# Blocks of 64 slots on two halves of the array's columns, in a two-layer graph network with routed experts

## The chip, the cores and the metric

The kernel runs on 1 core of one Trainium2 chip. The metric is the device time of one launch in microseconds (us); the time of a kernel is the median of its runs. The profile is one separately recorded execution; its span goes from the first to the last instruction on the core.

The engines are called as in the profile: PE (TensorE, matrix products and transposes), PEld (its weight loads), DVE (VectorE), ACT (ScalarE), POOL (GpSimd) and SP (SyncE, which only issues transfers). An engine's name with a q (SPq, ACTq, POOLq) stands for the instructions with which it issues DMAs.

## What is computed

N = 625 tokens of D = 768 numbers pass through two layers. Each layer adds to x a graph part and an attention part, and then the output of routed experts:

```python
edge_index = jnp.stack([src, dst])                     # 10000 edges, 8 types
xn = layernorm(x)
x = x + L0_gnn(xn, edge_index, edge_type_8) + L0_mix(xn)     # two relational convolutions; linear attention
x = x + L0_ffn(layernorm(x))                                 # 8 experts, 768-192-384-768, two of them per token
xn = layernorm(x)
x = x + L1_gnn(xn, edge_index) + L1_mix(xn)                  # two graph attentions; linear attention
x = x + L1_ffn(layernorm(x))                                 # 8 experts, 768-1152-768, two of them per token

# one relational convolution: mean over the incoming edges of each type, then a product per type
mean = segment_sum(x[src], dst * 8 + etype) / max(count, 1)
out = einsum('nri,rio->no', mean.reshape(N, 8, -1), W) + x @ root + b

# the experts (layer 1; layer 0 has two hidden layers and a bias on its scores)
probs, idx = top_k(softmax(x @ router_w + router_b), 2)
out = sum over e of gates[:, e] * (gelu(x @ w1[e] + b1[e]) @ w2[e] + b2[e])
```

All products are fp32, but for the neighbour sums, in which x is split into three bf16 parts.

## The kernel before

**Common parts.** Tokens stand as NB = 5 groups of T = 125. All matrix products write PSUM tiles called `ps`, [128, 2, 512] fp32, of which there are four in turn; `evac(dst, ps, i)` copies one out, on ACT for even i and on DVE for odd i (on ACT that is the line L163). `wpool` has five buffers named `w` for weight slabs of 1152 KB, loaded on SP's queue by `slabs` and `slab_tiles`; a load waits until an older slab's buffer is free, and what is queued behind it on SP waits too. Four large buffers (`work`, `features`, x's own, and `pair` of the relational layers) are used for one thing after another. Contents that are needed later are stored to `aside_d` in DRAM and read back by `recall` on ACT's queue (L981): `hid` (L808, SP's queue) in the first relational layer, x (L1124, SP's queue) in the second.

**Relational layers.** `rgcn` (from L847) is called twice, once per convolution. For each of seven relations it makes six neighbour-sum tiles (L853: bf16 products of the parts of x with the table of edge counts), scales and mixes them on DVE (L882 to L888), mixes quarters of the weight matrix on POOL (L874 to L878), and makes Strassen's seven products of half-size matrices. Each of the seven has three column slices of 128, so there are 21 products u of three steps of k each (L900), two of which share a PSUM tile: 11 tiles per relation, u0 = 0, 2, ..., 20. For relation 0 a tile is copied by `evac(total, ps, u0 // 2)`, so ACT and DVE alternate; for the others DVE adds it to the totals (L906). Totals 0 to 11 lie in `sums`, totals 12 to 20 in `more`, the first half of `pair`. `sums` overlays `place(2)`: in the first convolution that is `work`, which holds `hid` until L808 has stored it; in the second it is x's buffer, which holds x until L1124 has stored it. The eighth relation and the root product go through plain products; before them eight DVE operations (L921 to L931) combine the totals m1 to m7, and the last of them to read `sums` (L924, which the trace has behind L925) precedes the recall into `work` (`acc = back()`).

`counts` (L826 to L836) builds in the first layer the tile `cnt` of edge counts on POOL's queue, and stores it on ACT's queue (L834) for the second layer. ACT's queue is in order with ACT's own copies: where L834 waits for `cnt`, so do the copies behind it.

**Experts.** `Dispatch` (L360 to L435) gives each (token, expert) pair a slot. It ranks the tokens of each expert, counts the blocks of 128 slots that an expert needs (`nblk`, from the comparison of the expert's count with `steps` = 0, 128, ..., 512), gives each expert its first block (`first`), and writes for every block the expert (`es_i`), the token row of every slot (`idx`) and, in `gates`, the weight of every slot. These are products of one-hot tables, with one column per block. All this stands between the last score (L305, L431 is the last of its DVE operations that the first gather needs) and the first gather. NS = 17 blocks are enough for any routing; the first NU = 13 are run always, the other four in a branch, taken only if the chip counts more than 13 (L1217 in layer 0, L1520 in layer 1).

A block of layer 0 (`block0`, L1160 to L1203) loads its expert's weights on SP (`w12` for w1 and w2, three buffers; w3 in a `w` buffer), gathers 128 token rows (POOL), transposes them, and makes three products with transposes and a Gelu between them; its rows are multiplied by the gates and added to the sums in DRAM by an indirect DMA on POOL. `blocks0` runs the six steps of the blocks in a staggered order, each block three steps behind the one before. A block of layer 1 (`block1`, L1485 to L1517) takes three slabs of w1 (pool `moe`, six buffers) and three of w2 (`w`, five buffers), makes the first product in three column groups of 384 (L1498, 18 products), copies each out (L1501), transposes it, applies Gelu on ACT, and makes the second product in two column groups (L1511, 18 products). Blocks run one after the other.

In the attention of layer 0, the products L757 and L772 already write the two halves of the output partitions (0 to 63 and 64 to 127) in turn, each from a stationary of 64 columns.

The functions that the change touches, and what calls them:

## Time and profile before

| | |
|---|---|
| median of 3 runs | 2432.52 us (2432.51 to 2446.29) |
| the profiled execution | 2438.95 us, span 2437.2 us, mean granted clock 0.968 |
| busy PE / DVE / ACT / POOL | 93% / 38% / 12% / 19% of the span |
| DMA | 313.13 MB, mean 128 GB/s |
| neighbour sums, L853 | 2880 products, 391.6 us |
| relational products, L900 | 504 products, 138.8 us |
| expert products of layer 1, L1498 and L1511 | 468 each, 160.3 and 155.2 us |
| gathers of expert blocks, L487 | 26 (13 per layer) |

How to read the profile: the span is cut into 40 equal slices, and a row of digits gives the busy share of an engine in each, in tenths; the row DMA is the mean share of the core's 16 DMA engines. In a row of a timeline the first two numbers are the start in the span and the duration in us, followed by engine, line, operation, output <- inputs, partitions x elements and type, and the number of instructions that were merged (x16); [0.94 <-ACT xT L163] is the engine's idle time before it and what ended it. In a table of windows a row gives the stretch, the length and the sum over engines, and then the busy time and number of instructions of PE, PEld, DVE, ACT, POOL and SP; its last three columns are the mean granted clock, the busy share of the DMA engines and the GB/s that they moved. An fp32 product appears as two instructions (passes), so L1498's 468 products of 384 columns are 13 blocks times 18 products times two passes.

### The profile page before, as it was taken

The page shows a single profiled execution, that of the slowest core. Times are in us where ns is not written, and L with a number is a line of the kernel's source. Part 1 is how long each engine was busy: PE and PEld are TensorE (multiplying, and loading weights), DVE is VectorE, ACT ScalarE, POOL GpSimd, SP SyncE. Part 2 cuts the span into 40 slices and gives each one's busy share as a digit, 9 for nine tenths or more (in the row PEclk, how much of TensorE's full clock was granted, in tenths as well). Part 3 has the DMA queues.
Part 4 walks back from the last instruction along what each step waited for, and adds up shares of the span by engine and source line. Part 5 has one row for each costly group of instructions (what it writes and reads, how often), then busy time and mean ns, then how long its engine had stood idle before and what let it go on. Part 6 is the DMA issues. An engine that isn't in the chain of part 4 may idle for free. (4 is left out here: it accounts for less than half of the span.)

```text
span 2437.2 us, 24793 instructions
## 1 busy us (share of the span) xinstructions
PE 2270.4 (93%) x10116; PEld 1506.7 (62%) x10116; DVE 931.3 (38%) x1902; ACT 284.4 (12%) x583; POOL 467.0 (19%) x257
## 2 busy tenths in 40 slices
PE   7999979999999999999999797899999996999997
PEld 4666557777776567777776564455676554555554
DVE  7554143344334233344433422614673534211110
ACT  2111000000001000000000112213551201111110
POOL 1676532232220022222200121000000200010010
PEclk9999999999999999999999698999999998999998
DMA  9435395444422051111100997011003201988783
GB/s 360 84 53 55 76 249 139 122 129 134 131 61 77 12 183 60 62 58 53 33 32 26 296 312 205 13 71 72 1 24 105 72 13 31 396 319 314 275 310 120
DMA packets 153022, 313.13 MB, mean 128 GB/s; under 512 B 49070, under 2 KB 69938, under 8 KB 152864
## 3 DMA queue, kind: packets, MB, share of 16 engines
q1 hardware_dynamic: 91784, 234.38, 27.4%
q0 software_dynamic: 52384, 51.64, 10.9%
q10 hardware_dynamic: 8728, 25.38, 3.1%
q8 instruction: 85, 1.39, 0.2%
q14 instruction: 41, 0.34, 0.0%
HBM read 250.27 MB, written 64.76 MB: 129 GB/s over the span
## 5 line engine op out<-in xcount | busy, mean ns | idle before, releaser
L853 PE MATMUL ps<-cnt,parts 125*128 125x314 bf16 x2880 | 391.6, 299 | 7.2 <-DVEq L1038 4.9
L853 PEld LDWEIGHTS <-parts 125*128 125x128 bf16 x2880 | 283.0, 98 | 115.4 <-issue 10.5
L609 POOL DMA_INDIRECT table<-val,idx x80 | 162.2, 2028 | 132.8 <-DMA table<-val,idx 58.4
L1498 PE MATMUL ps<-w,xT 128*128 128x384 f32 x468 | 160.3, 493 | 13.2 <-ACT xT L163 6.6
L1511 PE MATMUL ps<-w,hT 128*128 128x384 f32 x468 | 155.2, 486 | 0.0
L900 PE MATMUL ps<-pair,w 128*128 128x314 f32 x504 | 138.8, 434 | 7.6 <-ACT work L163 7.6
L874 POOL TENSOR_TENSOR features<-w 128x1152 f32<-128x1152 f32 x14 | 37.3, 2666 | 526.0 <-issue 352.4
L487 POOL DMA_INDIRECT xg<-tokens,d_idx x26 | 26.3, 1011 | 544.3 <-PE ps L499 252.3
L1498 PEld LDWEIGHTS ps<-w,xT 128*128 128x128 f32 x468 | 86.7, 192 | 69.0 <-ACT xT L163 8.4
L900 PEld LDWEIGHTS ps<-pair,w 128*128 128x128 f32 x504 | 97.2, 193 | 46.9 <-ACT work L163 8.1
L1511 PEld LDWEIGHTS ps<-w,hT 128*128 128x128 f32 x468 | 87.8, 190 | 58.3
L187 PE MATMUL ps<-w,hT 128*125 128x384 f32 x360 | 117.8, 486 | 0.0
L187 PEld LDWEIGHTS ps<-w,hT 128*125 128x125 f32 x360 | 67.1, 188 | 46.9
L163 ACT COPY features<-ps 128x628 f32<-128x628 f32 (+1 forms) x15 | 10.5, 703 | 729.7 <-PE ps L853 728.9
L1312 PE MATMUL ps<-xl,pT 125*125 125x256 f32 (+1 forms) x300 | 81.0, 426 | 12.7 <-ACT pT L163 8.8
L906 DVE TENSOR_TENSOR pair<-ps,pair 128x628 f32<-128x628 f32 (+1 forms) x60 | 44.8, 746 | 122.7 <-PE ps L900 122.7
L822 PE MATMUL ps<-w,features 128*125 128x384 f32 x240 | 82.7, 503 | 0.0
L1501 DVE COPY a<-ps 128x384 f32<-128x384 f32 x39 | 21.7, 557 | 151.2 <-PE ps L1498 151.2
L187 PE MATMUL ps<-w,features 128*125 128x384 f32 x240 | 79.3, 490 | 0.0
L1424 POOL TENSOR_TENSOR row<-row 128x768 f32<-128x768 f32 x1 | 1.9, 1918 | 401.7 <-ACT z L1295 401.7
L1312 PEld LDWEIGHTS ps<-xl,pT 125*125 125x125 f32 x300 | 56.2, 191 | 34.4 <-ACT pT L163 10.3
L196 PE MATMUL ps<-features,w 128*128 128x313 f32 x288 | 77.4, 427 | 0.0
(374 smaller groups left out, 3349.8 us busy)
## 6 DMA issues: line engine op xcount, KB each, us to landing
w<-in_L_ffn_w_dram SPq DMA_DIRECT2D x78, 1152.0 KB
w<-in_L_gnn_W_dram SPq DMA_DIRECT2D x34, 1152.0 KB
w<-in_L_ffn_W_dram SPq DMA_DIRECT2D x13, 1152.0 KB
table<-zero SPq DMA_DIRECT2D x32, 400.0 KB
cnt<-table POOLq DMA_DIRECT2D x16, 800.0 KB, 7.9
edges<-cnt POOLq DMA_DIRECT2D x8, 1600.0 KB, 15.9
w<-in_L_ffn_W_dram SPq DMA_DIRECT2D x13, 576.0 KB
w<-in_L_mix_W_qkv_dram SPq DMA_DIRECT2D x6, 1152.0 KB
```

The costliest lines, as they stand in the source:

```text
L187: nc.tensor.matmul(ps[:T, h, :width], xT[:, k, blk(b)], w_of(k)[:, h * width : (h + 1) * width], start=(k == 0), stop=(k == nk - 1))
L196: nc.tensor.matmul(ps[:width, h, :NH], w_of(k)[:, c0 : c0 + width], xT[:, k, h * NH : (h + 1) * NH], start=(k == 0), stop=(k == nk - 1))
L487: nc.gpsimd.indirect_dma_start(out=dst, out_offset=None, in_=table_d, in_offset=bass.IndirectOffsetOnAxis(ap=rows, axis=0))
L609: scatter = nc.gpsimd.indirect_dma_start(out=table_of(g, j), out_offset=bass.IndirectOffsetOnAxis(ap=idx[:, j : j + 1], axis=0), in_=val[: ...
L822: nc.tensor.matmul(ps[:T, h, :384], aggs[:, k, blk(b)], w_of(k)[:, h * 384 : (h + 1) * 384], start=(k == 0), stop=(k == KC - 1))
L853: nc.tensor.matmul(ps[:, h, :HC], parts[:, b, i, k * 128 : (k + 1) * 128], cnt[:T, b, h * HC : (h + 1) * HC], start=(b == 0 and i == 0), s ...
L874: nc.gpsimd.tensor_add(wmix[:, 1], b11, b12)
L900: nc.tensor.matmul(ps[:, j, :HC], right[:, k, c : c + 128], left(k), start=(k == 0), stop=(k == K2 - 1))
L906: nc.vector.tensor_add(total, ps[:, :n, :HC], total)
L1312: nc.tensor.matmul(o, pT[:, j, :], xl[:, j, cols], start=(j == 0), stop=(j == NB - 1))
L1498: nc.tensor.matmul(ps[:, 0, :384], xT[:, k, :], w1_of(k)[:, q * 384 : (q + 1) * 384], start=(k == 0), stop=(k == KC - 1))
L1511: nc.tensor.matmul(ps[:, h, :384], hT[:, k, :], w2_of(k)[:, h * 384 : (h + 1) * 384], start=(k == 0), stop=(k == 8))
```

## The change

Blocks of two kinds. `steps` now begins at 64, so an expert whose last, partial block holds up to 64 slots gets a half block for it (numbers 13 to 20), and a whole block (0 to 12) where it holds more. `nblk`, `first` and `last` have two rows, one per kind, and `jump` and `rest` move the slots of a rest to their half block's number. The lists are written out: ten whole blocks and three half blocks (13, 14, 15) are always run, in the order RUN; the other three whole and five half blocks (MORE) in the branch, which is taken if the chip counts more than ten whole or more than three half blocks. The tables of blocks have 21 columns for 17.

A half block uses 64 slots as stationary and gives the array's two column halves two different groups of output columns, so the results stand on partitions 0 to 63 and 64 to 127. Its output tile has 128 rows of 384 numbers, and its scatter adds to half rows of the sums, with addresses `idx2`; the products that make `idx2` and the half blocks' gates are repeated for both halves. In layer 0 half blocks take part in the staggered order; in layer 1 the half block's first product comes between its whole neighbour's first and second product, and its own second product after that.

Relational layers. Totals 0 to 8 now go to `more` (in `pair`), totals 9 to 20 to `sums`, and the tiles are u0 = 0, 2, 4, 6, 8 (one product), 9, 11, ..., 19. For relation 0 `evac` gets u0, so the first five tiles go to ACT and the other six to DVE. The store of x before the second convolution is issued on ACT's queue, not SP's.

```diff
-NU = 13
-NS = 17
+NPB = 13
+NHB = 8
+NS = NPB + NHB
+RUN = (0, 1, 2, 13, 3, 4, 5, 14, 6, 7, 8, 15, 9)
+MORE = (10, 11, 12, 16, 17, 18, 19, 20)
+NUP, NUH = 10, 3
...
+            nblk = pool.tile([128, 2, 8], F32, name="d_nblk", bufs=1)
+            nc.vector.tensor_reduce(nblk[:, 0, :], over, AX.X, OP.add)
+            whole = pool.tile([128, 8], F32, name="d_whole", bufs=1)
+            nc.vector.tensor_scalar(whole, nblk[:, 0, :], 128.0, None, op0=OP.mult)
+            nc.vector.tensor_tensor(nblk[:, 1, :], rank[:, NB, :], whole, op=OP.is_gt)
...
+            jump = pool.tile([128, 8], F32, name="d_jump", bufs=1)
+            nc.vector.tensor_sub(jump, first[:, 1, :], nblk[:, 0, :])
+            nc.vector.scalar_tensor_tensor(jump, jump, float(NPB), first[:, 0, :], op0=OP.add, op1=OP.subtract)
+            rest = pool.tile([T, NB, 8], F32, name="d_rest", bufs=1)
+            nc.vector.tensor_tensor(rest, rank[:T, :NB, :], whole[:T, None, :].to_broadcast([T, NB, 8]), op=OP.is_ge)
+            nc.vector.tensor_mul(rest, rest, jump[:T, None, :].to_broadcast([T, NB, 8]))
+            nc.vector.tensor_add(rest, rest, first[:T, 0, None, :].to_broadcast([T, NB, 8]))
             pos = pool.tile([T, NB, 8], F32, name="d_pos", bufs=1)
...
+            nc.vector.scalar_tensor_tensor(pos, rest, 128.0, rank[:T, :NB, :], op0=OP.mult, op1=OP.add)
...
+            for h in (slice(0, 64), slice(64, 128)):
+                for c in range(2 * NB):
+                    nc.tensor.matmul(ps[h, 1, : 2 * NHB].rearrange("p (i s) -> p i s", i=2), lane_hot[:, c, :64],
+                                     put[:, :, c // NB, c % NB, NPB:], start=(c == 0), stop=(c == 2 * NB - 1))
...
+            behind(nc.vector.tensor_scalar(many, last[0:1, 0, 7:8], float(NUP), None, op0=OP.is_gt))
+            behind(nc.vector.scalar_tensor_tensor(self.used, last[0:1, 1, 7:8], float(NUH), many, op0=OP.is_gt, op1=OP.add))
...
+            behind(nc.vector.scalar_tensor_tensor(self.idx2, ps[:, 1, :NHB], 2.0, row2, op0=OP.mult, op1=OP.add))
...
+    def half_rows(table_d):
+        return table_d.rearrange("r (h d) -> (r h) d", h=2)
+    sides = [slice(0, 64), slice(64, 128)]
+    def half_slot_columns(src):
+        ps = ps_tile()
+        sl = ps.rearrange("p a c -> p (a c)")[:, : KC * 64].rearrange("p (k c) -> p k c", c=64)
+        for k in range(KC):
+            nc.tensor.transpose(sl[:, k, :], src[:, k * 128 : (k + 1) * 128], ident[:64, :64])
+        return sl
...
-            def of_product(i):
-                return sums[:, 3 * i : 3 * i + 3, :] if i < 4 else more[:, 3 * i - 12 : 3 * i - 9, :]
+            def of_products(u0, n):
+                return more[:, u0 : u0 + n, :] if u0 < 9 else sums[:, u0 - 9 : u0 - 9 + n, :]
...
-                for u0 in range(0, 21, 2):
+                for u0 in (0, 2, 4, 6, 8, 9, 11, 13, 15, 17, 19):
...
-                    n = min(2, 21 - u0)
+                    n = 1 if u0 == 8 else 2
...
-                    total = sums[:, u0 : u0 + n, :] if u0 < 12 else more[:, u0 - 12 : u0 - 12 + n, :]
+                    total = of_products(u0, n)
                     if r == 0:
-                        evac(total, ps[:, :n, :HC], u0 // 2)
+                        evac(total, ps[:, :n, :HC], u0)
...
-            nc.sync.dma_start(by_token(aside_d[2]), x)
+            nc.scalar.dma_start(by_token(aside_d[2]), x)
...
+            def block0_half(b, w1, w2, w3):
+                i = b - NPB
+                xg = moe.tile([128, D], F32, name="xg", bufs=4)[:64]
+                gather(xg, tokens_d[0], idx[:64, b : b + 1])
+                xT = moe.tile([128, KC, 128], F32, name="xT", bufs=3)[:, :, :64]
+                evac(xT, half_slot_columns(xg), b)
...
+                for k in range(KC):
+                    for j, p in enumerate(sides):
+                        nc.tensor.matmul(ps[p, 0, :96], xT[:, k, :], w1[:, k, j * 96 : (j + 1) * 96],
+                                         start=(k == 0), stop=(k == KC - 1))
+                a1 = moe.tile([128, 192], F32, name="a1")
+                nc.vector.tensor_copy(a1[:, :96], ps[:, 0, :96])
...
+                for k in range(2):
+                    for p, c in zip(sides, (slice(0, 256), slice(256, 384))):
+                        nc.tensor.matmul(ps[p, 0, : c.stop - c.start], h1[:96, k, :64], w2[:, k, c],
+                                         start=(k == 0), stop=(k == 1))
...
+                y = moe.tile([128, D], F32, name="y")[:, :384]
+                ps = ps_tile()
+                for k in range(3):
+                    for j, p in enumerate(sides):
+                        nc.tensor.matmul(ps[p, 0, :384], h2[:, k, :64], w3[:, k, j * 384 : (j + 1) * 384],
+                                         start=(k == 0), stop=(k == 2))
...
+                nc.vector.tensor_scalar(y, ps[:, 0, :384], gates[1][:, i : i + 1], None, op0=OP.mult)
+                scatter_add(half_rows(sums_d[0]), y, places_of.idx2[:, i : i + 1])
...
-            blocks0(range(NU))
+            blocks0(RUN)
             w1_of = slabs(a["L1_gnn_W1"], 1024, 2)
-            with tc.If(nc.values_load(used, min_val=0, max_val=NS) > NU):
-                blocks0(range(NU, NS), moe)
+            with tc.If(nc.values_load(used, min_val=0, max_val=2) > 0):
+                blocks0(MORE, moe)
...
+                i = b - NPB
+                gather(xg[:64], tokens_d[1], idx[:64, b : b + 1])
+                evac(xT[:, :, :64], half_slot_columns(xg[:64]), b)
+                ps = ps_tile()
+                for k in range(KC):
+                    for h in range(2):
+                        for p, c in zip(sides, (slice(h * 320, (h + 1) * 320), slice(640 + h * 256, 896 + h * 256))):
+                            nc.tensor.matmul(ps[p, h, : c.stop - c.start], xT[:, k, :64], w1_of(k)[:, c],
+                                             start=(k == 0), stop=(k == KC - 1))
+                a1 = moe.tile([128, 640], F32, name="a1_half", bufs=1)
+                nc.vector.tensor_copy(halves(a1[64:, :512]), ps[64:, :, :256])
+                nc.vector.tensor_copy(halves(a1[:64, :]), ps[:64, :, :320])
+                ps = ps_tile()
+                for c in range(4):
+                    nc.tensor.transpose(ps[:, 0, c * 128 : (c + 1) * 128], a1[:, c * 128 : (c + 1) * 128], ident)
+                nc.tensor.transpose(ps[:, 1, :64], a1[:64, 512:640], ident[:64, :64])
+                for c in range(9):
+                    at = ps[:, 1, :64] if c == 4 else ps[:, 0, c % 5 * 128 + c // 5 * 64 :][:, :64]
+                    nc.scalar.activation(hT[:, c, :64], at, AF.Gelu, bias=c1[:, b, c : c + 1])
+                yield
+                ps = ps_tile()
+                for k in range(9):
+                    for j, p in enumerate(sides):
+                        nc.tensor.matmul(ps[p, 0, :384], hT[:, k, :64], w2_of(k)[:, j * 384 : (j + 1) * 384],
                                          start=(k == 0), stop=(k == 8))
                 if not gates:
-                    gates.append(gate())
-                nc.vector.tensor_scalar(halves(y), ps[:, :, :384], gates[0][:, b : b + 1], None, op0=OP.mult)
-                scatter_add(sums_d[1], y, idx[:, b : b + 1])
-
-            for b in range(NU):
-                block1(b)
-            with tc.If(nc.values_load(used, min_val=0, max_val=NS) > NU):
-                for b in range(NU, NS):
-                    block1(b)
+                    gates.extend(gate())
+                nc.vector.tensor_scalar(y[:, :384], ps[:, 0, :384], gates[1][:, i : i + 1], None, op0=OP.mult)
+                scatter_add(half_rows(sums_d[1]), y[:, :384], places_of.idx2[:, i : i + 1])
+            def blocks1(bs):
+                run = {b: block1(b) for b in bs}
+                for i, b in enumerate(bs):
+                    if b < NPB or i == 0:
+                        next(run[b])
+                        within = i + 1 < len(bs) and b < NPB <= bs[i + 1]
+                        if within:
+                            next(run[bs[i + 1]])
+                        next(run[b], None)
+                        if within:
+                            next(run[bs[i + 1]], None)
+                    elif bs[i - 1] >= NPB:
+                        next(run[b])
+                        next(run[b], None)
+            blocks1(RUN)
+            with tc.If(nc.values_load(used, min_val=0, max_val=2) > 0):
+                blocks1(MORE)
```

## The prediction

> **What bounds the kernel now.** I read the page's engine and slice rows, then the windows of the two expert stages, the timeline there and at the starts of the relational layers, and the rows of the attention products that already use halves of the array.
>
> ```profile
> PE 2270.4 (93%) x10116; PEld 1506.7 (62%) x10116; DVE 931.3 (38%) x1902; ACT 284.4 (12%) x583; POOL 467.0 (19%) x257
> PE   7999979999999999999999797899999996999997
> DMA  9435395444422051111100997011003201988783
> ```
> TensorE is the bound nearly throughout, so what shortens its stream or removes one of its waits counts. DMA is also full in two stretches: the first expert stage (1362 to 1503 us) and the second (2077 to 2420).
>
> ```profile
> 1440.00:1445.00 5.00, 5.00 (x21) 3.35 (x21) 0.36 (x1) 0.00 (x0) 0.00 (x0) 1.00 1.06 313
> 2150.00:2155.00 5.00, 5.00 (x17) 2.94 (x16) 0.00 (x0) 0.00 (x0) 0.00 (x0) 1.00 0.31 83
> 2155.00:2160.00 5.00, 3.68 (x16) 2.26 (x15) 1.88 (x2) 0.00 (x0) 1.44 (x2) 1.00 0.96 378
> 2170.00:2175.00 5.00, 5.00 (x19) 3.03 (x18) 0.56 (x1) 1.06 (x4) 0.00 (x0) 1.00 1.03 413
> 2175.00:2180.00 5.00, 5.00 (x17) 2.95 (x16) 0.00 (x0) 0.00 (x0) 0.00 (x0) 1.00 0.14 52
> ```
> The last three columns are clock, DMA share and GB/s. In the first stage DMA is never idle; in the second it rests for some 5 us of every 26, waiting for a weight buffer (five `w` tiles; a block takes three for w2).
>
> ```profile
> 2132.85 5.43 PE L1498 MATMUL ps<-w,xT 128*128 128x384 f32 x16 [0.94 <-ACT xT L163]
> 2146.84 10.49 PE L1511 MATMUL ps<-w,hT 128*128 128x384 f32 x32
> 2395.49 5.43 PE L1498 MATMUL ps<-w,xT 128*128 128x384 f32 x16 [0.94 <-ACT xT L163]
> 133.84 2.33 PE L772 MATMUL ps<-phi_q,kv 128*64 128x313 f32 x16 [0.23 <-DVE kv L766]
> 145.19 2.38 PE L757 MATMUL ps<-phi_k,x 125*64 125x256 f32 x20
> ```
> A second-stage block lasts (2395.49 - 2132.85)/10 = 26.3 us. An fp32 product is two passes; L1511's 32 passes give (10.49 - 0.49)/31 = 0.323 us for 384 columns, 0.84 ns a column. L772 and L757 write the two halves of the output partitions in turn, from 64-column stationaries. Less the last pass's duration, L772 takes (2.33 - 0.43)/15 = 0.127 us per 313-column pass, where 0.263 would be serial; L757 (2.38 - 0.38)/19 = 0.105 against 0.215. So two halves overlap fully.
>
> ```profile
> 355.57 3.34 PE L900 MATMUL ps<-pair,w 128*128 128x314 f32 x12
> 365.75 0.68 ACT L163 COPY work<-ps 128x628 f32<-128x628 f32 x1 [136.71 <-DMA aside<-work]
> 365.78 0.33 ACTq L834 DMA_DIRECT2D counts<-cnt  x1
> 366.49 9.54 PE L900 MATMUL ps<-pair,w 128*128 128x314 f32 x24 [7.58 <-ACT work L163]
> 847.57 0.30 SPq L1124 DMA_DIRECT2D aside<-x  x1
> 868.02 2.67 POOL L874 TENSOR_TENSOR features<-w 128x1152 f32<-128x1152 f32 x1 [173.58 <-DMA w<-in_L_gnn_W_dram]
> 883.09 6.71 PE L900 MATMUL ps<-work,w 128*128 128x314 f32 x18 [3.20 <-POOL w L877]
> ```
> First relational layer: four PSUM tiles are full at 358.9 and none can be emptied, since `sums` overlays `work`, whose store lands at 365.7. Second: TensorE waits 3.2 us for mixed weights that landed late behind the store of x.
>
> **How many blocks there will be.** Evaluating the reference's routers on its inputs gives, per expert, 0, 366, 6, 167, 0, 2, 624, 85 slots in the first layer and 0, 0, 1, 579, 0, 262, 408, 0 in the second. In 128s that is 13 blocks each, as the trace has it (L1202 and L1515 x13). With rests up to 64 taken as halves it is 10 whole and 3 half blocks in both layers: exactly the unconditional list, so the conditional one stays untaken.
>
> **Second expert stage.** A half block's first product has 6 k x 2 x 2 passes of 320 columns beside 256 in the other half: 24 x 0.269 = 6.5 us. The second: 18 x 0.323 = 5.8. Eleven transposes (a whole block's fifteen take 0.82 + 3 x 0.49 = 2.3): 1.4. The wait for xT, as now: 1.0. Changes between whole and halved array: some six at 0.1 (L757's last pass starts near 147.19, full-array L196 at 147.50, 0.1 beyond that pass's 0.215): 0.6. Sum 15.3, so 11.0 less than 26.3, three times: -32.9. Without changes of array and with shorter transposes it is 14.6 (-35); with 0.2 us for each of seven changes and 1.9 us for two DVE copies that nothing covers, 18 (-25). Weight bytes stay. A whole block and its half are queued on SP with six w2 tiles; the sixth, and the next block's w1 behind it, waits until the whole block has read w2's first tile for the last time, two thirds through its second product (S2). From there to the next first product is 4 + 5.8 + 2 = 12 us; the queue owes four tiles of 1.18 MB by then, 2.95 us each at 400 GB/s plus some 3 us to land (L353's load issued at 1513.77 is read at 1517.48), and the scatter's traffic: 14.6 to 16.6 us; the last tile is needed 2.6 us in, at 14.6. So a stall of 0 to 2 us per pair: +3 (0 to +6). On POOL the half block's scatter follows the whole one's by 6 us, and a scatter lands in 8.9, so POOL waits some 3 us; the gathers behind it run a block ahead: 0. Net -30.
>
> **First expert stage.** Ten blocks from 1388.8 to 1489.1 are 10.0 us each. Half block: L1180's products are 12 pairs of 96 columns, 0.081 us of streaming, but two weight loads (L757's loads come every 0.096 us): 1.8 for now 1.9. w2 4 x 0.215 = 0.9 (1.3); w3 6 x 0.323 = 1.9 (3.9); transposes 1.1 (1.75); waits as now 1.3, array changes 0.5. Sum 7.5: -7.5 in all. DMA, saturated, saves only half a gather and scatter per half block, so I keep -6 (-3 to -10).
>
> The Trainium skill (TensorEngine Tiling (Array Packing), Key Properties) says that changing the tiling mode drains TensorE, which speaks against short half blocks. This trace agrees in kind, but shows 0.1 us at L196. If by that rule each change cost a whole tail (0.379 - 0.215 us at L757), the six half blocks would give back some 7 us for changes, where the sum holds 3.5.
>
> **Routing, on the path twice.** TensorE idles from choice to gather. Seven dependent DVE operations are added before `pos` (1349.49 to 1349.75 to 1349.98: 0.23 us a step): 1.6; slot_hot, put, pre and first are wider (21 slots for 17) and es8 is split: 0.6; the casts to `used` and idx2 come after idx. +2.4 per layer, +5 (4 to 7). The 20 extra half matmuls there run while DVE goes on, free; in gates() the same 20 stand in TensorE's stream: 10 now take 0.42, so +0.85, with the wider DVE work +1 per layer: +2 (1 to 3). Wider bias tables: DVE has idle time beside the first block, 0. Four iotas at the start: POOL is idle there (3.46 of the first 40 us); uncovered, 0.7.
>
> **Relational layers.** In the first, nine products (14 us) now go to `pair` and five evacuations to ACT, so the store at 365.7 no longer stops them. But ACT's queue holds L834, which waits for counts that also landed at 365.78. With one evacuation ahead of it TensorE gains half a tile, 1.6 us; with two, 4.8; with three or more all 7.6 plus the 3.2 us of low clock after the gap (24 passes in 9.54 where 0.264 each, as at 355.57, makes 6.3). Take -5.5 (-1.6 to -10.8). In the second, x's store moves from the head of SP's queue to ACT's, so weights share DMA with it and land up to 10 us earlier; gone would be the 3.2 + 0.4 us wait and 2.0 us of low clock (18 passes in 6.71, not 4.75). On ACT the store stands before or among ten small loads from 844.9, 0.3 us each, and ACT's first evacuation comes at 878: 0. But POOL's five sums (2.6 us each) then overlap DVE's 857 to 872 us work; in the first layer such a series held one DVE operation for 14.5 us and cost TensorE 4 us (340 to 345.5). Take -3.5 (-5.5 to +2). The Trainium skill (DMA: Bandwidth & Descriptors, Issuing engines are not separate DMA queues) says all issuers share the same engines, so the move buys no bandwidth; the 362 to 377 GB/s from 855 to 870 agree that they were full. If the weights came no sooner by it, this term is 0. At each layer's end the last reader of `sums` becomes L931 instead of L924, so ACT issues the recall at 743.05, not 738.88; it took some 17 us to land and is needed 20 us after: +0.7 per layer, +1.5 (0 to +3).
>
> **Sum.** -30 - 6 + 5 + 2 - 5.5 - 3.5 + 1.5 = -36.5. The profiled execution took 2438.95 us (span 2437.2), 6.4 above the median 2432.52; so 2402.5 on that execution, **2396** against the median.
>
> **Rivals.** *Everything hides*: ACT is ahead of L834 by three, no weight stalls, first stage at -9: about -52, **2380**. For: ACT is idle there; against: L834 came after a single evacuation now. Chance 0.15. *Transfers take it back*: the first stage, with share 1.06, gains nothing and each pair stalls 6 us: -36.5 + 6 + 15 = -15, **2417**. For: the full queue; against: 5 us of rest per block now. 0.12. *The halves do not overlap here* (the change does not do what it says): half blocks cost what whole ones do, the rest is -0.5 and four drains add little: **2432**. Against it stand L757 and L772. 0.07. *Slower: the conditional list runs.* Place: L1520's (or L1217's) branch. It decides once the chip counts more than 10 whole or 3 half blocks; expert 3 in the second layer has 67 slots beyond 512, so three tokens routed otherwise make its rest a fourth half. Price there 3 x 26.3 + 5 x 15.3 = 155: **2551**. For: the margin of three; against: 13 blocks were needed as evaluated. 0.06. The forecast, with 2385 to 2410 as its own range, has 0.60.
>
> **Numbers.** Without the branch and the serial case (0.13), and with the edge of the transfers, the range is 2378 to 2419. A measurement tells about 1% (24 us) from no change. Faster than 2408 are the forecast, the first rival and a sixth of the transfers: 0.77. Within 1% lie the rest of those and the serial case: 0.17. Slower: 0.06.
>
> **What would show it.** Right: pairs at the new L1498-like lines with passes near 0.13 to 0.16 us; whole plus half in 41 to 43 us at 2140 to 2190; no TensorE wait on `work` near 360; L431's successor some 2.4 us later after the scores. Wrong: TensorE waits of the half block or its successor on DMA `w`; a pass interval near 0.3; more than 26 gathers on POOL.

## The result and the profile after

The changed kernel takes 2404.86 us in the median of 3 runs (2404.84 to 2412.28), before 2432.52: the ratio is 0.9891, 95% interval 0.9867 to 0.9915, so 21 to 32 us faster. The forecast was 2396 with a range of 2378 to 2419. The profiled execution took 2404.86 us, span 2403.1. The kernel before, run again beside every experiment, had medians of 2433.2, 2435.0, 2433.8 and 2434.2.

Three rows of the changed kernel's profile page:

```profile
PE 2227.3 (93%) x10262; PEld 1473.7 (61%) x10262; DVE 932.2 (39%) x1930; ACT 278.0 (12%) x579; POOL 467.1 (19%) x261
PE   7999989999999999999999697799999998799996
DMA  9435395444432051111101699112003200779785
```

TensorE's busy time fell by 43.1 us (2270.4 to 2227.3) and the span by 34.1 (2437.2 to 2403.1); TensorE remains the bound. Gathers stay at 26, so the conditional lists did not run. The timeline of the changed kernel in the second expert stage, one whole block and its half (start, duration):

```profile
2126.58 0.82 PE L558 MATMUL ps<-ident,xg 128*128 128x128 f32 x6
2128.34 5.43 PE L1613 MATMUL ps<-w,xT 128*128 128x384 f32 x16 [0.94 <-ACT xT L177]
...
2140.81 0.58 PE L550 MATMUL ps<-ident,xg 64*128 64x64 f32 x6
...
2142.09 6.64 PE L1641 MATMUL ps<-w,xT 128*64 128x320 f32 x48
...
2148.79 0.69 DVE L1644 COPY a_half<-ps 64x512 f32<-64x512 f32 x1 [6.80 <-PE ps L1641]
2149.50 0.82 DVE L1645 COPY a_half<-ps 64x640 f32<-64x640 f32 x1
2150.46 0.63 PE L1648 MATMUL ps<-ident,a_half 128*128 128x128 f32 x4 [1.73 <-DVE a_half L1645]
...
2151.22 11.88 PE L1626 MATMUL ps<-w,hT 128*128 128x384 f32 x36
...
2163.03 6.03 PE L1657 MATMUL ps<-w,hT 128*64 128x384 f32 x36
...
2168.98 0.88 PE L558 MATMUL ps<-ident,xg 128*128 128x128 f32 x6
```

Pair to next block: 2168.98 - 2126.58 = 42.4 us. With 26.3 for the whole block, the half block costs 16.1, forecast 15.3. Its 48 and 36 passes come every 0.138 and 0.168 us where a whole block's come every 0.323. The new wait is short: 1.73 us for two DVE copies one after the other.

The two traces, aligned by TensorE's instructions (their start in the one against the other), give this ledger; "unchanged" is code that both kernels have:

| place | forecast | trace after - before |
|---|---|---|
| up to the first relational layer (unchanged) | 0 | -0.3 |
| first relational layer, relation 0 | -5.5 | -5.7 |
| ends of the two convolutions (recall) | +1.5 | +1.2 + 1.3 |
| start of the second convolution | -3.5 | +3.7 - 5.7 |
| routing, both layers | +5 | +2.6 + 2.9 |
| first expert stage to the first read of its sums, gates | -6 + 1 | -7.1 |
| graph attention of the second layer (unchanged) | 0 | -2.0 |
| second stage, first two blocks, gates | +1 | +4.4 |
| second stage, the rest | -30 | -30.1 |
| sum | -36.5 | -34.8 |

The sum goes up to TensorE's last products; the spans, which also hold the last scatter, differ by 34.1. Both are differences of two single executions. The medians differ by 27.7.

### The profile page after: what moved, and what is told of

Same layout as the page of the kernel before. It is cut to its first block, busy times and chain, and to the rows that moved or that the text cites. A ratio compares the mean times of both kernels' runs of the same rounds, so it can differ in the third digit from the quotient of the medians.

```text
span 2403.1 us, 25088 instructions
## 1 busy us (share of the span) xinstructions
PE 2227.3 (93%) x10262; PEld 1473.7 (61%) x10262; DVE 932.2 (39%) x1930; ACT 278.0 (12%) x579; POOL 467.1 (19%) x261
## 5 line engine op out<-in xcount | busy, mean ns | idle before, releaser
L912 PEld LDWEIGHTS <-parts 125*128 125x128 bf16 x2880 | 283.2, 98 | 121.4 <-issue 16.1
L1613 PE MATMUL ps<-w,xT 128*128 128x384 f32 x360 | 126.3, 502 | 11.3 <-DVE xT L175 6.7
L1626 PE MATMUL ps<-w,hT 128*128 128x384 f32 x360 | 119.2, 487 | 0.0
L1613 PEld LDWEIGHTS ps<-w,xT 128*128 128x128 f32 x360 | 68.0, 196 | 56.0 <-DVE xT L175 8.1
L1626 PEld LDWEIGHTS ps<-w,hT 128*128 128x128 f32 x360 | 67.5, 190 | 45.0 <-issue 0.3
L536 POOL DMA_INDIRECT sums<-y,d_idx x26 | 41.1, 1581 | 220.1 <-DVE y L1630 77.3
L1425 PEld LDWEIGHTS ps<-xl,pT 125*125 125x125 f32 x300 | 56.2, 191 | 34.1 <-ACT pT L177 10.3
```

Source lines behind the costliest of these rows:

```text
L536: nc.gpsimd.indirect_dma_start(out=table_d, out_offset=bass.IndirectOffsetOnAxis(ap=rows, axis=0), in_=src, in_offset=None, compute_op=OP.add)
L912: nc.tensor.matmul(ps[:, h, :HC], parts[:, b, i, k * 128 : (k + 1) * 128], cnt[:T, b, h * HC : (h + 1) * HC], start=(b == 0 and i == 0), s ...
L1425: nc.tensor.matmul(o, pT[:, j, :], xl[:, j, cols], start=(j == 0), stop=(j == NB - 1))
L1613: nc.tensor.matmul(ps[:, 0, :384], xT[:, k, :], w1_of(k)[:, q * 384 : (q + 1) * 384], start=(k == 0), stop=(k == KC - 1))
L1626: nc.tensor.matmul(ps[:, h, :384], hT[:, k, :], w2_of(k)[:, h * 384 : (h + 1) * 384], start=(k == 0), stop=(k == 8))
```

## The experiments

**The two parts apart.** `rel_only` is the kernel before with these lines and the totals' new places, `half_only` the changed kernel with them undone:

```diff
+                for u0 in (0, 2, 4, 6, 8, 9, 11, 13, 15, 17, 19):
...
+                        evac(total, ps[:, :n, :HC], u0)
...
+            nc.scalar.dma_start(by_token(aside_d[2]), x)
```

> The kernel before with only the relational part of the change (totals 0 to 8 to the pair buffer, the new list of tiles, evacuations 5 on ACT and 6 on DVE, the store of x on ACT's queue). Theory, from the ledger of the two traces: -7.3 us at the first relational layer, -2 at the second, +1.2 and +1.3 where the recall comes later, so about -7 us, 2425.5. In its trace TensorE shows no wait on work near 360 us, and a wait of some 8.5 us ahead of the first neighbour sums of the second convolution, 3.6 more than before. Rival: the -7.3 is only a shift of the half-clock periods, and the change is worth 0 to -3 us, 2430 to 2432.

Measured: 2431.9 us, ratio 0.9988 (0.9976 to 0.9999): -2.9 us (-0.2 to -5.8). The expected -7 is missed; the time is in the rival's range of 0 to -3. That the rest was a shift of half-clock periods, as the rival had it, no run shows.

> The changed kernel with the relational part undone: blocks of 64 alone. Theory: the parts add, so this keeps the rest of the measured -27.7 us, about -21, 2411.5; the wait on work near 360 us (7.6 us) and the wait of 4.9 us at the second convolution are back. Rival: the parts share cover (the later part gains less once the earlier is in), then it takes all of -25 to -28, 2405 to 2407.

Measured: 2409.74 us, ratio 0.9898 (0.988 to 0.9917): -24.8 us (-20 to -29), between the theory's -21 and the rival's -25 to -28. The two parts add to -27.7, so they are additive as far as this resolves. TensorE in `rel_only` at the two places, then in `half_only`:

```profile
366.40 3.51 PE L901 MATMUL ps<-pair,w 128*128 128x314 f32 x6 [4.63 <-ACT pair L163]
...
847.48 26.55 PE L853 MATMUL ps<-cnt,parts 125*128 125x314 bf16 x180 [7.80 <-DVEq L1039]
873.86 9.67 PE L901 MATMUL ps<-work,w 128*128 128x314 f32 x36
```

```profile
367.73 8.37 PE L959 MATMUL ps<-pair,w 128*128 128x314 f32 x24 [7.00 <-ACT work L177]
...
848.04 26.38 PE L912 MATMUL ps<-cnt,parts 125*128 125x314 bf16 x180 [5.07 <-DVEq L1097]
...
882.99 6.71 PE L959 MATMUL ps<-work,w 128*128 128x314 f32 x18 [3.19 <-POOL w L936]
```

The wait for the store of hid (7 us) becomes one for ACT (2.1 in the changed kernel, 4.6 in `rel_only`), the wait for mixed weights (3.19) goes, and the wait ahead of the second convolution grows from 5 to 8.

**Why that wait grows: the queue of the store.** Three kernels move the store of x. `store_sp` and `store_pool`:

```diff
-            nc.scalar.dma_start(by_token(aside_d[2]), x)
+            nc.sync.dma_start(by_token(aside_d[2]), x)      # store_sp; store_pool: nc.gpsimd
```

> The changed kernel with the store of x before the second convolution back on SP's queue. Theory: with the store on ACT's queue the weight slabs are issued 10 us earlier (838 us), fill the DMA engines while the cores pass the conditional branch, and the branch's code, which comes by DMA too, arrives later: TensorE waits 8.5 us there instead of 4.9. So here the wait ahead of the first neighbour sums falls back to about 4.9, and the wait on the mixed weights (3.2 us) with its low clock returns: -3.6 and +5.7 in the trace, +2 in all. Rival: the longer wait has nothing to do with the slabs and stays at 8.5; then this costs the full 5.7.

> The changed kernel with that store on POOL's queue, so neither SP's nor ACT's queue carries it. The slabs start as early as in the changed kernel. Theory (the slabs delay the branch): the wait ahead of the first neighbour sums stays near 8.5 us, the time within 2 us of the changed kernel. Rival (ACT's queue, with the store and ten loads, delays the branch): the wait falls to 4.9 and the time by 3.6.

Measured: 2406.26 us (ratio 0.9882, 0.9852 to 0.9913) and 2405.43 us (0.9885, 0.9857 to 0.9912); neither differs from the changed kernel. So the move of the store, which `store_sp` alone takes back, is worth nothing that these runs resolve. In the traces the waits differ clearly: `store_sp` 4.79 us, `store_pool` 7.09. So it is the slabs in flight, not ACT's queue, though 7.09 is 1.4 below the changed kernel's 8.48. The changed kernel there, and `store_sp`:

```profile
838.46 1.45 SPq L164 DMA_DIRECT2D w<-in_L_gnn_W_dram  x3
839.37 0.96 DVE L1054 TENSOR_TENSOR x<-x,row 125x768 f32<-125x768 f32 x1
846.51 0.51 ACTq L1184 DMA_DIRECT2D aside<-x  x1
...
846.82 26.77 PE L912 MATMUL ps<-cnt,parts 125*128 125x314 bf16 x180 [8.48 <-DVEq L1098]
```

```profile
843.21 26.64 PE L912 MATMUL ps<-cnt,parts 125*128 125x314 bf16 x180 [4.79 <-DVEq L1098]
869.91 5.02 PE L960 MATMUL ps<-work,w 128*128 128x314 f32 x18
878.13 6.71 PE L960 MATMUL ps<-work,w 128*128 128x314 f32 x18 [3.19 <-POOL w L937]
```

L1098 is the conditional branch that leads past the repair code. The trace's packets show what comes ahead of the resumption: one packet of 8 KB on the queue that the profile's page lists as instruction (q14), so presumably the code behind the branch. It starts 0.72 to 0.74 us after DVE's last operation in the kernel before, `half_only` and `store_sp`, but 4.30 us after it in the changed kernel, 3.59 in `rel_only` and 3.00 in `store_pool`; TensorE resumes 2.1 to 2.4 us behind its start in all of them. Windows of the changed kernel (last three columns: clock, DMA share, GB/s) show what the DMA engines do meanwhile; in `store_sp` the same windows have 0, 11 and 39 GB/s.

```profile
838.00:840.00 2.00, 0.34 (x2) 0.00 (x0) 1.59 (x2) 0.00 (x0) 0.00 (x0) 1.00 0.22 35
840.00:842.00 2.00, 0.00 (x0) 0.00 (x0) 0.33 (x1) 0.00 (x0) 0.00 (x0) 0.98 0.82 304
842.00:844.00 2.00, 0.00 (x0) 0.00 (x0) 0.00 (x0) 0.00 (x0) 0.00 (x0) 0.50 1.03 416
```

A kernel that keeps the slabs out of the branch, built on `pipelined` (below):

```diff
+            nc.sync.dma_start(by_token(aside_d[2])[:, NB - 1, :], x[:, NB - 1, :])
             slabs_ = slab_tiles(a["L0_gnn_W2"][0], D, 3)
-            nc.scalar.dma_start(by_token(aside_d[2]), x)
+            nc.scalar.dma_start(by_token(aside_d[2])[:, : NB - 1, :], x[:, : NB - 1, :])
```

> The pipelined kernel, with the store of x split: the last of its five groups of tokens goes first on SP's queue, ahead of the weight slabs, the other four stay on ACT's queue. So the slabs cannot start before x is complete, but no large store is ahead of them. Theory: while the cores pass the branch the DMA engines are free, the packet with the branch's code comes 0.7 us after DVE's last operation (3.0 to 4.3 where slabs were in flight), and TensorE waits 4.9 us ahead of the second convolution instead of 8.1 to 8.5; the slabs land early enough for POOL's five sums, so the 3.2 us wait of the kernel before does not return: -3.5 against the pipelined kernel, 2386.5. Rival 1: the branch takes its time whatever the transfers do, and the wait stays above 7. Rival 2: the slabs land too late, the wait of 3 us on mixed weights returns, and nothing is gained.

Measured: 2390.68 us (ratio 0.9813, 0.9792 to 0.9834), no better than `pipelined`, as rival 2 had it. Its trace has both halves of the answer: the packet comes 0.74 us after DVE's last operation and the branch is fast, as the theory of the branch foretold, and the weights are late.

```profile
841.88 26.32 PE L912 MATMUL ps<-cnt,parts 125*128 125x314 bf16 x180 [4.84 <-DVEq L1098]
868.04 4.92 PE L960 MATMUL ps<-work,w 128*128 128x314 f32 x18
875.59 4.74 PE L960 MATMUL ps<-work,w 128*128 128x314 f32 x11 [2.63 <-POOL w L937]
```

In both places tried the slabs cost some 3 us: loaded during the branch, they go with a longer wait there; loaded behind it, they delay POOL's sums.

**Do the halves overlap, and by what?** `serial_sides` changes the order alone, in both products of the second stage's half blocks:

```diff
-                for k in range(9):
-                    for j, p in enumerate(sides):
+                for j, p in enumerate(sides):
+                    for k in range(9):
                         nc.tensor.matmul(ps[p, 0, :384], hT[:, k, :64], w2_of(k)[:, j * 384 : (j + 1) * 384],
```

> The changed kernel with the half blocks of the second layer writing first all of one column half and then all of the other, the same products in another order. Theory: two halves overlap only where neighbouring products go to different halves; then the first product takes 24 x (0.269 + 0.215) = 11.6 us for now 6.6, the second 36 x 0.323 = 11.6 for 6.0, so 10.6 us per half block and +32 in all, 2437. Rival: the halves gain by something else than alternation (shorter weight loads, fewer columns), and the order makes no difference, 2405.

Measured: 2434.14 us, ratio 0.9999 (0.9986 to 1.0012): the whole gain is gone.

```profile
2145.80 10.80 PE L1642 MATMUL ps<-w,xT 128*64 128x320 f32 x48
...
2159.08 13.57 PE L1626 MATMUL ps<-w,hT 128*128 128x384 f32 x36
2172.58 10.59 PE L1658 MATMUL ps<-w,hT 128*64 128x384 f32 x36
```

The two products take 10.80 and 10.59 us for 6.64 and 6.03, together 8.7 us more per half block. In the first two of the three half blocks a half-clock period is added, which makes the neighbour's 36 passes of L1626 last 13.57 us for 11.88; these two cost 10.4 us more, the third 8.7. The starts of the single passes in the traces show the overlap: in the changed kernel the 36 passes of the second product start 0.007 and 0.316 us apart in turn, in `serial_sides` 0.323, as in a whole block, but for some pairs where the one half follows the other. That is why they take less than the 11.6 us expected. The halves overlap only where neighbouring products go to different halves.

**The first stage.** `half_l1` counts the first layer in blocks of 128 again:

```diff
-            nc.vector.tensor_tensor(over, rank[...], steps, op=OP.is_gt)
+            nc.vector.tensor_tensor(over, rank[...], steps if router.layer else steps0, op=OP.is_gt)
...
-            blocks0(RUN)
+            blocks0(range(13))
```

> The changed kernel with half blocks in the second layer only; the first layer counts in blocks of 128 again and runs 13 whole ones. Theory: a half block of the first stage saves 3.4 us (four blocks in 36.7 us where they took 40.1), three save 10, and the end of the stage gives 1.3 back, so this is 9 us slower than the changed kernel, 2414. Rival 1, the prediction's term: transfers leave only 6, 2411. Rival 2: transfers take all of it, 2405.

Measured: 2410.01 us, ratio 0.9907 (0.9891 to 0.9923), 3 to 5 us slower than the changed kernel by ratios and medians, but the intervals overlap; its profiled execution, the longest of its six, shows more (span 2417.5). The prediction's -6 is nearest, though the run excludes neither rival 2 (nothing) nor much of the theory. That the stage moves faster is seen in the changed kernel, where four blocks with one half take 1428.67 - 1391.86 = 36.8 us; before, four take 40.15 (1396.98 to 1437.13):

```profile
1391.86 0.59 PE L550 MATMUL ps<-ident,xg 64*128 64x64 f32 x6
...
1428.67 0.58 PE L550 MATMUL ps<-ident,xg 64*128 64x64 f32 x6
```

Three halves would then save 10. I thought that scatters give part of it back, through DVE products that wait for them:

```diff
-                y = moe.tile([128, D], F32, name="y")
+                y = moe.tile([128, D], F32, name="y", bufs=4)     # in both kinds of block
```

> The changed kernel with four buffers for the output rows of the first expert stage instead of two. In the changed kernel two of DVE's output products there wait 5.7 and 4.3 us for a scatter to land, since a half block's scatter follows its neighbour's after 7 to 8 us and not 10, and DVE's queue then holds a copy that TensorE waits for (1.3 us) ahead of a half-clock period at 1484 us. Theory: these waits go and with them 2 to 4 us at the end of the stage, 2402. Rival: the scatters themselves, one after the other on POOL, set the end of the stage, and nothing changes.

Measured: 2405.46 us (ratio 0.9884, 0.9864 to 0.9905). The waits of DVE for a scatter are gone from the list (they were 5.7 and 4.3 us), and the time is the same: that theory falls, the rival fits. TensorE's wait for the first tokens read back from the sums, in the kernel before, the changed kernel and `y_bufs`:

```profile
1520.83 1.48 PE L173 MATMUL ps<-ident,part 125*128 125x125 f32 x6 [10.70 <-DVE part L218]
```

```profile
1510.93 1.49 PE L187 MATMUL ps<-ident,part 125*128 125x125 f32 x6 [13.80 <-DVE part L232]
```

```profile
1511.26 1.48 PE L187 MATMUL ps<-ident,part 125*128 125x125 f32 x6 [15.93 <-DVE part L232]
```

So 3.1 of the 10 us that the half blocks save are given back here. In `y_bufs` TensorE's product ahead of this wait starts 3.4 us earlier (1490.73 for 1494.17), and the wait ends no sooner. The last scatter starts at 1496.50 in the changed kernel and at 1496.41 in `y_bufs`, in both released by the landing of the one before; in the kernel before it was released by DVE's product. So the chain of scatters sets the end of the stage by the traces, but no run took the chain itself away.

**The counts' store.**

```diff
-                nc.scalar.dma_start(counts_d[r], cnt)
+                nc.gpsimd.dma_start(counts_d[r], cnt)
```

> The changed kernel with the store of the counts in the first layer issued on POOL's queue, behind the transfer it waits for, so ACT's copies do not stand behind it. Theory: in the changed kernel two evacuations came ahead of that store and TensorE then waited 2.1 us for ACT, with the lower clock after it; both go, -2 to -4 us at the first relational layer. Rival: the wait goes over to the store of hid, which lands at 365.7 and holds the totals in work; then the same 2 us are lost there and nothing changes.

Measured: 2416.86 us, ratio 0.9927 (0.99 to 0.9954), 12 us slower than the changed kernel. At the place meant the products run on with no wait, but that is no test of the theory or of the rival: relation 0 began 18 us later (332.51 for 314.31), and the last store of `hid` was issued at 310.39 where the changed kernel has it at 340.9, so `work` had had 30 us longer to be freed. Two places of its trace:

```profile
332.51 25.68 PE L912 MATMUL ps<-cnt,parts 125*128 125x314 bf16 x180 [23.14 <-issue]
...
373.46 9.69 PE L960 MATMUL ps<-pair,w 128*128 128x314 f32 x36
```

Why the first relation, whose counts POOL builds, came later was not settled.

**A version that beats both.** `late_half` moves the half block's transposes behind the first column group of its neighbour's second product; its two new stops, without the loop that calls them in turn:

```diff
                     for h in range(2):
+                        if h:
+                            yield
...
                 nc.vector.tensor_copy(halves(a1[:64, :]), ps[:64, :, :320])
+                yield
                 ps = ps_tile()
```

> The changed kernel with the half block's transposes and Gelu moved, in the second stage, behind the first column group of its whole neighbour's second product, so that the two DVE copies ahead of them lie beside TensorE's work. Theory: the wait of 1.7 us ahead of these transposes goes, three times, -5 us. Rival: another wait takes its place (PSUM tiles, or the Gelu that then comes too late for the half block's second product), and nothing changes.

Measured: 2400.78 us, ratio 0.9868 (0.9845 to 0.9892); the 1.7 us waits are gone, and its trace gains 4.7 us from the first pair to the end. The medians differ by 4 us, and the intervals overlap. `pipelined` also transposes the next block's rows ahead of the last part of the current block:

```diff
                     evac(xT, to_slot_columns(xg, KC), b)
+                    yield
...
+                    if after:
+                        next(after)          # the next block's gather, transposes and xT
+                    next(h or w, None)       # the last part of this block or of its half
```

> The kernel with the late transposes of half blocks, and beside it the next block's gathered rows transposed and copied ahead of the last part of the block that runs, so that in the second stage no first product waits for its xT. Theory: the late transposes give -5 as they did alone; the waits for xT in the second stage, twelve of 0.9 to 1.9 us, give another 13; the half-clock period that followed the longest of them goes too, -1.7. Together -18 to -20 against the changed kernel, 2386. Rival: the weight transfers, which rest less the shorter the blocks, become the bound, and TensorE waits for w instead: no better than the late transposes alone, 2400.

Measured: 2390.11 us, ratio 0.9815 (0.9796 to 0.9833), 15 us below the changed kernel, clear of its interval, where 18 to 20 were expected. Its TensorE waits from 2067 to 2380 us, and below them the changed kernel's:

```profile
PE ps L1614 <- DMA w<-in_L_ffn_w_dram: 2.5, 3, 1.6
PE ps L1614 <- ACT xT L177: 0.9, 1, 0.9
PE ps L356 <- DVE x L359: 0.8, 1, 0.8
PE ps L1619 <- DVE a L1617: 0.7, 1, 0.7
```

```profile
PE ps L1613 <- DVE xT L175: 6.7, 5, 1.9
PE ps L1648 <- DVE a_half L1645: 5.1, 3, 1.7
PE ps L1613 <- ACT xT L177: 4.6, 5, 0.9
PE ps L1618 <- DVE a L1616: 0.7, 1, 0.7
```

17.1 us of waits become 4.9. These 12.2 us and one half-clock period (1.7 us) make up most of the 15. The first waits for weights appear, the rival's, though small: 2.5 us in all.

**The spread.**

> The changed kernel once more, for the spread of its executions beside the two that follow. The traces so far differ by up to 7 us ahead of 360 us, where the programs are the same (the first neighbour sums start between 311 and 314 us, and a DVE operation is held 9 to 14.5 us beside five sums on POOL), and by single half-clock periods of 3.4 us. Theory: executions of this kernel spread over some 10 us, 2400 to 2412, and the 6.4 us by which the profiled execution of the kernel before lay above its median are of this kind. Rival: the spread belongs to the kernel before alone.

Measured: 2405.16 us (2400.91 to 2416.63, 6 runs), ratio 0.9893 (0.987 to 0.9915); the kernel before spread from 2427.36 to 2440.03 beside the experiments, with one run of 2446.29 beside the result. The theory holds: both kernels spread over more than 10 us. So the profiled execution of the kernel before, at 2438.95, lay near the upper end of its spread, that of the changed kernel at its median.

## Why the prediction was nearly right, and where it was 8 us too good

The direction, the main mechanism and the range held; the size was -36.5 against a measured -27.7 (-26 to -29 by the ratio and the later medians).

*Second expert stage, -30: right, in part by luck.* 24 x 0.269 = 6.5 came out as 6.64, the second product's 5.8 as 6.03. Six changes of array, costed at 0.6, find some 0.2 us: 0.58 + 6.64 + 1.73 + 0.63 + 0.27 + 6.03 = 15.9 of the 16.1 us. The sum had a wait of 1.0 for xT; the one that came was 1.73 for two DVE copies, which stood only in the pessimistic case. The transfers' stall, +3, did not come: no wait of TensorE on `w` in the list above. So a half block that cost 0.8 more, three times, and a stall that did not come all but cancelled: -32.9 + 2.4 gives -30.5, measured -30.1.

*First expert stage, -6: right within what was resolved, but by other terms.* The half block saves more than forecast, 3.4 us for 2.5: the 24 passes of its first product take 1.21 us, where the working had 1.8 (two loads of 0.096 for each of 12 pairs would even be 2.3). What took some of it back was not the transfers' share of 1.5 us in that sum, but 3.1 us at the first read of the sums, for which the prediction had no term. The medians and ratios show 3 to 5 in all.

*Routing, +5: right.* 2.6 and 2.9.

*First relational layer, -5.5: right in the trace, by the case of two evacuations.* L893, the old L834, stood behind two copies on ACT (at 350.12 and 353.49), its wait ended at 365.57, and TensorE waited 2.1 us.

```profile
353.49 0.68 ACT L177 COPY pair<-ps 128x628 f32<-128x628 f32 x1 [2.69 <-PE ps L960]
...
365.57 0.33 ACTq L893 DMA_DIRECT2D counts<-cnt  x1
...
366.67 2.75 PE L960 MATMUL ps<-pair,w 128*128 128x314 f32 x6 [2.11 <-ACT pair L177]
```

*Second relational layer, -3.5: the step that failed.* The prediction saw that the weights would come up to 10 us earlier, and they did: the wait for mixed weights, its low clock and the 0.4 us are gone (-5.7). It did not ask what the earlier transfers would collide with: the wait at the branch. That is +3.6 us here (8.48 for 4.91), and the traces with and without slabs in flight show it. So the term came to -2.0 in the ledger, inside its range, whose upper end, +2, stood there for POOL's sums beside DVE and not for this; by the median of `store_sp`, the one run that takes the store's move alone back, it came to about 1 us, which is not resolved.

*Gates, +1 in the second layer: the other step.* The entry of the second stage cost 4.4. The 20 extra products take 0.7 us, forecast 0.85. But the order of instructions in the built program now puts the last of the second block's six transposes behind the 24 passes of the first block's second product. The kernel before:

```profile
2098.45 0.85 PE L499 MATMUL ps<-ident,xg 128*128 128x128 f32 x6
...
2106.88 6.61 PE L1498 MATMUL ps<-w,xT 128*128 128x384 f32 x20
```

The changed kernel:

```profile
2090.09 0.77 PE L558 MATMUL ps<-ident,xg 128*128 128x128 f32 x5
...
2090.69 7.91 PE L1626 MATMUL ps<-w,hT 128*128 128x384 f32 x24
2098.44 0.27 PE L558 MATMUL ps<-ident,xg 128*128 128x128 f32 x1
...
2100.57 7.12 PE L1613 MATMUL ps<-w,xT 128*128 128x384 f32 x16 [1.86 <-DVE xT L175]
```

So the copy of xT, hidden before, is waited for, and a half-clock period follows from 2101.4 to 2104.9 (16 passes in 7.12 us for 5.43). All these are in `pipelined`'s gain.

*The sum against the median.* The prediction took 36.5 off an execution that was 6.4 us above its median and then 6.4 more to reach the median. On the spans it was wrong by 2.4 us; but the traced execution of the kernel before was a long one, and -2.3 of the ledger's -34.8 lie in code that both kernels have. The rows of the changed code add to -32.5, 4.8 more than the medians' -27.7. The two parts measured alone split this: the relational rows add to -5.2, `rel_only` gives -2.9 (forecast -7.5); the rows of the half blocks add to -27.3, `half_only` gives -24.8 (forecast -29). So of the 8.8 us by which the forecast was too good, some 4 are terms that the ledger shows mis-sized: the entry +3.4, the second relational layer +1.5, the recalls +1.0, the routing +0.5, the first stage -2.1. For the rest the cause stays open: both parts are worth less in the medians than in the two traces.

*The rivals.* "The halves do not overlap" is excluded by the passes. That `serial_sides` came to 2434, near this rival's 2432, does not prove its price: only the second stage's halves are serial there, the first stage's still overlap, and two half-clock periods are in it. "Transfers take it back" is excluded in the second stage, "everything hides" by the wait behind L893 and the time, and the conditional list did not run.

## What to carry to other kernels

With a stationary of 64 columns, two column halves nearly doubled the rate here as long as neighbouring products alternated between them; written one half after the other, the same products took 1.6 to 1.8 times as long, and the gain of the whole change was gone. An earlier transfer is not free because its own consumer waits less: look for what else waits for DMA at that moment, a branch among it. A stage that gets faster can end in a chain that does not: look at what follows the last product, here the scatters. A few added instructions can move others in the compiled order, so read the order after the change, not only the cost of what was added.

## What the runs showed of the hardware that was not expected

A wait at a branch can depend on data transfers: at the branch past the repair code it was 4.8 to 5.1 us in the traces where the DMA engines were all but idle and 7.1 to 8.5 us where weight slabs were in flight (416 GB/s in the changed kernel). In all of them one 8 KB packet on an instruction queue comes ahead of the resumption, 0.7 us after DVE's last operation in the first group and 3.0 to 4.3 us after it in the second.

The granted clock has two values in these traces, 1.0 and 0.5, and every half-clock stretch lasts a multiple of 3.4 us, but for the one that the end of the trace cuts. The Trainium skill (TensorE: Matmul & The Clock Gate, What's actually happening) describes a free-running window of about 3.4 us and a half clock after an idle one. The traces agree on the length, but the wait of 1.86 us at the entry of the second stage, far shorter than a window, was followed by a half-clock period in nine of the ten profiled executions that had it (all but `late_half`). Of the waits of 1.6 to 1.7 us ahead of the half blocks' transposes only two had one behind them, both in `serial_sides`, and the waits of 1.3 us between blocks had none. What decides is not settled.

Wide sums on POOL hold DVE: one DVE operation that takes 0.48 us alone lasted 14.27 us beside five sums on POOL in the changed kernel, 9.05 in `late_half`, 9.46 in `store_pool`. In every one of the 14 traces it ends 0.35 us behind the last of the five sums. The changed kernel and the seven kernels made from it that differ from it only further down run the same code up to there, and still in their nine traces the first neighbour sums start between 311 and 316 us and the first product of relation 0 between 335 and 344.
